# The first eight tiles of a graph kernel handled as two halves of four, with the attention vectors' products behind the first half

## The chip, the cores and the metric

The kernel runs on one core of one Trainium2 chip. The metric is the device time of one execution in microseconds. Five executions before the change gave a median of 1932.76 us, from 1931.08 to 1934.57 us.

The engines are named as in the profile: PE is TensorE (matrix products; PEld is its loading of weights), DVE is VectorE, ACT is ScalarE, POOL is GpSimd and SP is SyncE, which issues most of the DMAs here. A name with a small q behind it (SPq) is the queue of instructions of that engine. Each engine works through its own instructions strictly in order, and waits on semaphores for the others.

## What is computed

`x` holds 3125 nodes with 256 numbers each, `src` and `dst` the two ends of 103125 edges, sorted by `dst`. Four layers follow one another, each with a layer norm in front and a residual sum behind. The change lies at the start of the first, a three-layer graph attention:

```python
def _gat_layer(x, src, dst, W, al, ar, b, n_nodes):
    h = x @ W
    el = h @ al
    er = h @ ar
    e = jax.nn.leaky_relu(el[src] + er[dst], NEG_SLOPE)
    m = jax.ops.segment_max(e, dst, num_segments=n_nodes)
    ex = jnp.exp(e - m[dst])
    s = jax.ops.segment_sum(ex, dst, num_segments=n_nodes)
    alpha = ex / s[dst]
    out = jax.ops.segment_sum(alpha[:, None] * h[src], dst, num_segments=n_nodes)
    return out + b

x = x + _L0_gnn_ref(_layernorm(x, axis=-1), src, dst, ...)     # three _gat_layers
x = x + _L0_ffn_ref(_layernorm(x, axis=-1)[None], ...)[0]      # 16 experts, 2 for each node
x = x + _L1_gnn_ref(_layernorm(x, axis=-1), ...)
x = x + _L1_ffn_ref(_layernorm(x, axis=-1)[None], ...)[0]      # 8 experts, 1 for each node
```

## The kernel before

The nodes lie in 25 tiles of 128 (the last has 53), and two tiles make a group, so that there are 13 groups (`GROUPS`). The attention is computed densely: for every pair of tiles the number of edges between their nodes is counted into `counts`, and TensorE multiplies with these counts. Behind the layer norm, a tile needs its projection `h`, and two scores, which come out of the same product, because the weights `we` have two further columns, `W @ al` and `W @ ar`.

The front, which is what the change touches, is the part of `dense_attention` (line 1121) ahead of the loop over the three layers. In the order of the program it does this:

- `Locator` (line 1457) loads the first ends of the sorted list (an ACT DMA at line 1476) and makes two short lists of them on DVE (L1487, L1490). `load_nodes` loads `x` with six DMAs of four tiles and one for the last tile (L1668, L1671), on SP's queue: two in front of the weights' three DMAs (`attention_weights`, L1063 to L1065: `al` and `ar` into `wa`, `W` into `we`), the others behind them.
- `locator.find(0)` (line 1498) finds where the first part of the nodes begins in the list of edges: one large comparison on DVE (L1502), 33 small matmuls on PE (L1508), two small DVE operations (L1510, L1512), and two gathers of edges by POOL's own DMAs (L1523).
- `WARM` = 24 matmuls on PE follow (L1175). They multiply the comparison's result, so that they wait for L1502, and nothing reads what they make.
- `statistics(t0, n)` (line 1157) makes mean and variance of tiles on DVE (L1163, L1164). Those of tiles 4 and 5 come behind the comparison by a copy written for that (L1162).
- `spreads(t0, n)` (line 1166) makes the reciprocal spreads of some tiles: a square root on ACT (L1168) and a reciprocal on DVE (L1169).
- `turn(a)` (line 1178) normalises the two tiles of group a (L1184: the first on DVE, the second on POOL), transposes each with two PE matmuls into PSUM (L1188), and copies them back on ACT (L1190, `yT`).
- `products()` (line 1067) issues the DMA of the bias (L1068), and makes the two further columns of `we` in four DVE products with an accumulator each (L1074), behind a small copy that holds them back (L1071).
- The loop over the groups (line 1200) makes the statistics of tiles 8 to 24 in portions, their spreads in group 3 together with `locator.finish(0)` (DVE L1540 to L1550, ACT L1545, PE L1555, ACT L1558: it turns the gathered edges into keys for counting), turns the next group, and puts the present one: `Sources.put` (line 1103) multiplies on PE with `we` (L1111), clips the scores on DVE (L1114, `lr`), takes two exponentials on ACT (L1115, L1116), and scales the projection out of PSUM on ACT (L1118). From group 4 on each group also counts two pairs of windows (DVE L1594, PE L1606, ACT L1609).

The instructions of each engine are put in their order by a scheduler when the program is built. It starts from the order of the program and moves an instruction forward where its own times say that the engine would stand idle. The orders below are those of the built programs. Square root and exponential need different tables on ACT; a load of a table is inserted where the needed one isn't there.

Of the kernel before, what the change touches and what calls it, by code (L numbers as in the profile page):

```python
# [9 lines left out]
F32 = mybir.dt.float32  # L10
# [5 lines left out]
AF = mybir.ActivationFunctionType  # L16
OP = mybir.AluOpType
# [4 lines left out]
P = 128  # L22
# [4 lines left out]
D = 256  # L27
# [1020 lines left out]
EARLY = 8  # L1048
# [3 lines left out]
def attention_weights(tc, cp, one, layers, i, behind=None):  # L1052


    nc = tc.nc
    w, al, ar, b = layers[i]
    we = cp.tile([P, KD, D + 2], F32, name="we")
    at = cp.tile([P, 2, D], F32, name="wa")
    bt = cp.tile([P, D], F32, name="wb")
    if behind is not None:  # L1060
        for to in (we[:, 0], at[:, 0], at[:, 1], bt):
            nc.gpsimd.tensor_copy(to[:, 0:1], behind)
    nc.sync.dma_start(at[:, 0], spread(al, D))  # L1063
    nc.sync.dma_start(at[:, 1], spread(ar, D))
    nc.sync.dma_start(we[:, :, :D], w.rearrange("(k p) f -> p k f", p=P))  # L1065

    def products(behind=None):
        nc.sync.dma_start(bt, spread(b, D))  # L1068
        junk = one.tile([P, D], F32, name="wjunk")
        if behind is not None:  # L1070
            nc.vector.tensor_copy(junk[:, 0:1], behind)  # L1071
        for k in range(KD):
            for j in range(2):
                nc.vector.scalar_tensor_tensor(junk, we[:, k, :D], 1.0, at[:, j], op0=OP.mult, op1=OP.mult,  # L1074
                                               accum_out=we[:, k, D + j:D + j + 1])
    return we, bt, products
# [13 lines left out]
class Sources:  # L1090
# [9 lines left out]
        for to in (self.h[:, NT - 1], self.rho[:, NT - 1:], self.lr[:, :, NT - 1]):  # L1100
            self.nc.gpsimd.memset(to, 0.0)

    def put(self, pp, t, r, xTs, w, at=()):


        nc, n = self.nc, len(xTs)
        pss = []
        for i, xT in enumerate(xTs):
            ps = at[i] if i < len(at) else pp.tile([P, D + 2], F32, name="ps_m")
            for k in range(KD):  # L1110
                nc.tensor.matmul(ps[:r], xT[:, k], w[:, k], start=(k == 0), stop=(k == KD - 1))  # L1111
            pss.append(ps)
        for i, ps in enumerate(pss):
            nc.vector.tensor_scalar(self.lr[:r, :, t + i], ps[:r, D:], -HELD, HELD, op0=OP.max, op1=OP.min)  # L1114
        nc.scalar.activation(self.h[:r, t:t + n, D], self.lr[:r, 0, t:t + n], AF.Exp, scale=0.2)  # L1115
        nc.scalar.activation(self.rho[:r, t:t + n], self.lr[:r, 0, t:t + n], AF.Exp, scale=0.8)  # L1116
        for i, ps in enumerate(pss):
            nc.scalar.activation(self.h[:r, t + i, :D], ps[:r, :D], AF.Copy, scale=self.h[:r, t + i, D:])  # L1118


def dense_attention(tc, dram, counts, x_in, big, ident, eps, layers, src, dst, rows, high, make_router, over):
# [9 lines left out]
    nc = tc.nc  # L1131
    with tc.tile_pool(name="dw", bufs=1) as cp, tc.tile_pool(name="dwl", bufs=2) as wl, \
# [7 lines left out]
        we, bt, products = attention_weights(tc, wl, cp, layers, 0)  # L1140
        load_nodes(nc, x, x_in, EARLY)
        now = Sources(tc, big, small)
        with tc.tile_pool(name="dp", bufs=6) as pmp, tc.tile_pool(name="ds", bufs=2) as sp, \
# [10 lines left out]
            mv = small.tile([P, NT, 2], F32, name="mv")  # L1154
            rstd = small.tile([P, 2, NT], F32, name="rstd")

            def statistics(t0, n):
                for t in range(t0, t0 + n):
                    st = sp.tile([P, 6], F32, name="st")
                    if EARLY // 2 <= t < EARLY // 2 + 2:  # L1160

                        nc.vector.tensor_copy(st[:NHEAD, 0:1], locator.less[:NHEAD, 0, 0:1])  # L1162
                    nc.vector.bn_stats(st, x[:, t])  # L1163
                    nc.vector.bn_aggr(mv[:, t], st)  # L1164

            def spreads(t0, n):
                to = rstd[:, :, t0:t0 + n]
                nc.scalar.activation(to[:, 0], mv[:, t0:t0 + n, 1], AF.Sqrt, bias=eps)  # L1168
                nc.vector.reciprocal(to[:, 0], to[:, 0])  # L1169
# [3 lines left out]
            made = ap_.tile([P, 2, CHUNK], F32, name="acc")  # L1173
# [4 lines left out]
            def turn(a):  # L1178
                c, n = GROUPS[a]
                xTs = []  # L1180
                for j, q in enumerate(range(0, n, P)):
                    t, r = (c + q) // P, min(P, n - q)
                    xn = sp.tile([P, D], F32, name=f"y{j}")
                    (nc.gpsimd if j else nc.vector).tensor_scalar(xn, x[:, t], mv[:, t, 0:1], rstd[:, 0, t:t + 1],  # L1184
                                                                  op0=OP.subtract, op1=OP.mult)
                    to = turned[:, a % 2, j * D:(j + 1) * D]
                    for k in range(KD):
                        nc.tensor.transpose(to[:, k * P:(k + 1) * P], xn[:, k * P:(k + 1) * P], ident)  # L1188
                    xT = sp.tile([P, KD, P], F32, name=f"yT{j}")
                    nc.scalar.copy(xT, to.rearrange("p (k r) -> p k r", k=KD))  # L1190
                    xTs.append(xT[:, :, :r])
                return xTs

            statistics(0, EARLY)
            spreads(0, EARLY)
            xTs = turn(0)
            products(mv[:, EARLY - 1, 0:1])
            stats = list(range(EARLY, NT))
            ahead = list(pairs[0])
            for a, (c, n) in enumerate(GROUPS):  # L1200
                pairs_now = [ahead.pop(0) for _ in range(min(2, len(ahead)) if 2 * a >= EARLY else 0)]
                for pair in pairs_now:
                    counter.make(pair, 0)
                while stats and len(stats) > (NT - EARLY) * (EARLY // 2 - a - 2) // (EARLY // 2 - 1):
                    statistics(stats.pop(0), 1)
                if 2 * a == EARLY - 2:
                    spreads(EARLY, NT - EARLY)
                    locator.finish(0, pp, mv[:, NT - 1, 0:1])
                later = turn(a + 1) if a + 1 < len(GROUPS) else None
                now.put(pp, c // P, min(P, n), xTs, we, [made[:, a % 2, :D + 2]])  # L1210
                xTs = later
                for pair in pairs_now:
                    counter.add(kp, pair)
# [4 lines left out]
            for i in range(3):  # L1218
# [10 lines left out]
                else:  # L1229
                    nxt = Sources(tc, big, small)  # L1230
                    we_n, bt, products = attention_weights(tc, wl, cp, layers, i + 1, now.rho[:, NT - 1:])
# [81 lines left out]
                now = nxt  # L1313
# [441 lines left out]
```

## Time and profile before

| | |
|---|---|
| median of five executions | 1932.76 us |
| the profiled execution | 1931.46 us |
| its span (first to last instruction) | 1929.7 us |
| mean granted TensorE clock | 0.993 |
| PE busy | 1864.6 us, 97% of the span |
| DVE, ACT, POOL busy | 1002.6, 748.6, 297.3 us |
| PE busy from 0 to 13 us | 0 us of 13 |
| PE busy from 23 to 29 us and from 29 to 35 us | 4.36 us and 3.96 us of 6 |
| PE busy from 35 to 58 us | 22.53 us of 23 |

The times below count from the start of the span. In a row of the timeline the first number is the start, the second the time that the instructions in it took from the first start to the last end; then engine, line, operation, what is written and read, and the count; in brackets stands how long the engine was idle before, and what ended that. Instructions of one engine overlap by some ten nanoseconds, so that the step from one start to the next is a little shorter than the duration.

### The profile page before, as it was taken

Reading aid. Unit: us, or ns where it says so; the run is one execution under the profiler, and the core shown is the slowest. Engines: PE = TensorE matmul, PEld = TensorE weight load, DVE = VectorE, ACT = ScalarE, POOL = GpSimd, SP = SyncE. Lnnn points to the kernel's source line nnn. Section 1 sums busy time; section 2 is a strip of 40 time slices with the busy share of each in tenths; the row PEclk is TensorE's granted clock in tenths of the full one; section 3 lists DMA queues with packets and bytes.
Section 4 is the critical chain, followed back from the end, with each engine's and each line's share of the span. In section 5 each row is a group of like instructions: output and inputs, shape, how many; then the busy total and the mean of one; then the engine's idle time right before and its main releaser. Section 6 shows DMA issues by size and latency. Waiting matters only on the chain.

```text
span 1929.7 us, 27975 instructions
## 1 busy us (share of the span) xinstructions
PE 1864.6 (97%) x9466; PEld 1480.3 (77%) x9466; DVE 1002.6 (52%) x2909; ACT 748.6 (39%) x2254; POOL 297.3 (15%) x454
## 2 busy tenths in 40 slices
PE   6999999999999999999999989999989999999998
PEld 4788888887788888788888757777668887455887
DVE  6899888785555555567777722222235222334222
ACT  4867777672000011122222211111127999544221
POOL 4200000000000000022323322233310000132122
PEclk9999999999999999999999989999999999999999
DMA  4101113575100000011111165667540000633764
GB/s 124 32 21 53 41 67 121 209 282 236 58 1 1 1 1 3 9 56 45 44 45 45 39 200 151 188 176 240 125 105 1 1 1 1 229 137 143 215 209 137
DMA packets 103577, 182.96 MB, mean 95 GB/s; under 512 B 10054, under 2 KB 72741, under 8 KB 103392
## 3 DMA queue, kind: packets, MB, share of 16 engines
q1 hardware_dynamic: 72268, 124.32, 18.9%
q0 software_dynamic: 16016, 34.28, 6.5%
q10 hardware_dynamic: 15138, 22.44, 3.6%
q8 instruction: 80, 1.31, 0.3%
q14 instruction: 75, 0.61, 0.1%
HBM read 92.93 MB, written 90.17 MB: 95 GB/s over the span
## 4 chain that ended last, share of the span: by engine, by line
PE 87%; issue 5%; DMA 3%; ACT 3%; DVE 2%; POOL 1%; SPq 0%; ACTq 0%; POOLq 0%; DVEq 0%
PE acc L1263 40%; PE ps_h L762 9%; PE acc L1382 7%; PE ps_H L901 4%; PE ps_o L775 4%; PE ps_y L995 4%; PE acc_c L1606 4%; PE ps_m L1111 3%; DMA out_dram<-y,who 2%; PE ps_h L807 1%; PE ps_m L1365 1%; PE ps_rows L945 1%; PE acc L1385 1%; PE ps_cols L1022 1%; PE ps_o L819 1%
## 5 line engine op out<-in xcount | busy, mean ns | idle before, releaser
L1263 PE MATMUL acc<-big,pm 128*128 128x257 f32 (+1 forms) x3750 | 871.0, 382 | 4.7 <-DVE pm L1260 4.3
L1263 PEld LDWEIGHTS acc<-big,pm 128*128 128x128 f32 (+1 forms) x3750 | 680.5, 187 | 110.8 <-DVE pm L1260 9.6
L1260 DVE SCALAR_TENSOR_TENSOR pm<-tau,rho,counts 128x256 f32<-128x256 f32 (+1 forms) x975 | 437.3, 467 | 158.7 <-PE acc L1263 155.9
L762 PE MATMUL ps_h<-xsT,w 128*128 128x384 f32 x512 | 167.8, 486 | 0.5 <-ACT xsT L738 0.5
L1382 PE MATMUL acc<-msg,cr 128*128 128x512 f32 (+1 forms) x625 | 157.9, 403 | 0.1
L1594 DVE TENSOR_TENSOR ohk<-iota_k,key 128x1200 f16<-128x1200 f16 x196 | 151.5, 774 | 6.3 <-PE acc_c L1606 6.2
L762 PEld LDWEIGHTS ps_h<-xsT,w 128*128 128x128 f32 x512 | 97.2, 190 | 65.1 <-ACT xsT L738 0.7
L1382 PEld LDWEIGHTS acc<-msg,cr 128*128 128x128 f32 (+1 forms) x625 | 114.7, 185 | 29.2 <-ACT cr L1378 1.2
L1378 ACT ACTIVATE cr<-counts 128x256 fp32r<-128x256 uint8 (+1 forms) x325 | 130.5, 402 | 14.4 <-PE acc L1382 7.0
L1606 PE MATMUL acc_c<-ohk,ohs 128*128 128x200 f16 x1176 | 130.0, 249 | 1.4 <-ACT ohs L1591 1.4
L1590 ACT ACTIVATE far<-iota_s,low 128x128 f16<-128x128 f16 x360 | 123.6, 398 | 6.8 <-POOL far L1588 2.5
L1606 PEld LDWEIGHTS <-ohs 128*128 128x128 f16 x1176 | 105.0, 98 | 26.2 <-ACT ohs L1591 1.8
L995 PE MATMUL ps_y<-t_wd,hsT 128*128 x480 | 108.8, 380 | 0.4 <-ACT hsT L1023 0.4
L765 ACT ACTIVATE silu<-ps_h 128x384 f32<-128x384 f32 x64 | 31.4, 491 | 199.5 <-PE ps_h L762 199.5
L766 DVE TENSOR_TENSOR hid<-silu,ps_h 128x384 f32<-128x384 f32 x64 | 35.5, 554 | 136.3 <-PE ps_h L762 126.4
L1609 ACT CAST counts<-acc_c 128x400 uint8<-128x400 f32 x196 | 93.3, 481 | 32.7 <-PE acc_c L1606 32.0
L1243 ACT ACTIVATE tau<-ps_m 128x256 f32<-128x256 f32 (+1 forms) x39 | 14.1, 370 | 215.5 <-PE ps_m L1241 197.3
L995 PEld LDWEIGHTS ps_y<-t_wd,hsT 128*128 128x128 f32 x480 | 88.8, 190 | 11.6 <-ACT hsT L1023 0.6
L780 POOL DMA_INDIRECT sums<-y,who x48 | 75.0, 1562 | 131.4 <-DVE y L778 121.8
L901 PE MATMUL ps_H<-big,t_w 128*128 128x512 f32 (+1 forms) x224 | 93.1, 552 | 0.8 <-ACT H L903 0.5
L775 PE MATMUL ps_o<-w,hid 128*128 128x256 f32 x384 | 86.9, 379 | 0.0
L1594 DVE TENSOR_TENSOR ohs<-iota_s,low 128x512 f16<-128x512 f16 (+1 forms) x196 | 83.5, 426 | 0.0
(298 smaller groups left out, 1931.5 us busy)
## 6 DMA issues: line engine op xcount, KB each, us to landing
rows<-empty SPq DMA_DIRECT2D x16, 2564.0 KB, 15.0
w<-in_L_ffn_w_dram ACTq DMA_DIRECT2D x42, 512.0 KB, 7.5
hs<-rows SPq DMA_DIRECT2D x29, 641.0 KB, 4.1
w<-in_L_ffn_w_dram SPq DMA_DIRECT2D x30, 512.0 KB, 4.9
rows<-empty SPq DMA_DIRECT2D x16, 516.0 KB, 4.3
t_wd<-in_L_ffn_Wd_dram SPq DMA_DIRECT2D x8, 1024.0 KB, 12.5
xs<-rows SPq DMA_DIRECT2D x15, 387.0 KB, 5.2
bias<-in_L_ffn_bd_dram SPq DMA_DIRECT2D x30, 128.0 KB
```

The costliest lines, as they stand in the source:

```text
L762: nc.tensor.matmul(ps, w[:, k, j * P:(j + 1) * P], xsT[:, k], start=(k == 0), stop=(k == KD - 1))
L775: nc.tensor.matmul(ps, hid[:, j, q * P:(q + 1) * P], o[:, j], start=(j == 0), stop=(j == nh - 1))
L901: nc.tensor.matmul(ps[:, :n], a[:, k, j * P:(j + 1) * P], xnT[:, k, c:c + n], start=(k == 0), stop=(k == KD - 1))
L995: nc.tensor.matmul(ps, hsT[:, j], d[:, ds(e, 1), j, :].rearrange("p o f -> p (o f)"), start=(j == 0), stop=(j == nh - 1))
L1260: nc.vector.scalar_tensor_tensor(pm[:, :n], tau[:, :n], now.rho[:, s:s + 1], edges[:, s, :n], op0=OP.max, op1=OP.mult)
L1263: nc.tensor.matmul(acc[:r, j, :D + 1], pm[:, q:q + r], now.h[:, s], start=(s == 0), stop=(s == NT - 1))
L1378: nc.scalar.activation(cr[:, :n], edges[:, s, :n], AF.Copy, accum_out=seen[:, a * NT + s:a * NT + s + 1])
L1382: nc.tensor.matmul(acc[:r, j].rearrange("p h d -> p (h d)"), cr[:, q:q + r], msg[:, s].rearrange("p h d -> p (h d)"), start=(s == 0), stop ...
L1590: nc.scalar.activation(far[:, i], self.iota_s, AF.Abs, scale=-1.0, bias=self.low32[:, pair, i:i + 1])
L1594: nc.vector.tensor_tensor(to[:, i:].rearrange("p t (x u) -> p t x u", u=2), iota.rearrange("p (x u) -> p x u", u=2)[:, None].to_broadcast( ...
L1606: nc.tensor.matmul(acc[:, u], ohs[:, i], ohk[:, i], start=(t == 0), stop=(t == TW - 1))
L1609: nc.scalar.copy(to[:, :, d0 % PAIR:d0 % PAIR + 2 * WIN].rearrange("p s (u d) -> p u s d", u=2), acc.rearrange("p u (s d) -> p u s d", d=WIN))
```

## The change

`spreads` and `statistics` of the first eight tiles are made in two halves, tiles 0 to 3 and 4 to 7. `products` now stands behind the statistics of tile 3, not of tile 7, and ahead of the first `turn`. A tile `zero` is made out of the reciprocal spread of tile 7 times 0.0, and the exponentials of groups 0 and 1 take it as their bias, so that they come behind the second square root.

```diff
-    def put(self, pp, t, r, xTs, w, at=()):
+    def put(self, pp, t, r, xTs, w, at=(), zero=0.0):
...
-        nc.scalar.activation(self.h[:r, t:t + n, D], self.lr[:r, 0, t:t + n], AF.Exp, scale=0.2)
-        nc.scalar.activation(self.rho[:r, t:t + n], self.lr[:r, 0, t:t + n], AF.Exp, scale=0.8)
+        nc.scalar.activation(self.h[:r, t:t + n, D], self.lr[:r, 0, t:t + n], AF.Exp, bias=zero, scale=0.2)
+        nc.scalar.activation(self.rho[:r, t:t + n], self.lr[:r, 0, t:t + n], AF.Exp, bias=zero, scale=0.8)
...
-            statistics(0, EARLY)
-            spreads(0, EARLY)
+            half = EARLY // 2
+            statistics(0, half)
+            spreads(0, half)
+            products(mv[:, half - 1, 0:1])
             xTs = turn(0)
-            products(mv[:, EARLY - 1, 0:1])
+            statistics(half, EARLY - half)
+            spreads(half, EARLY - half)
+
+            zero = small.tile([P, 1], F32, name="zero")
+            nc.vector.tensor_scalar(zero, rstd[:, 0, EARLY - 1:EARLY], 0.0, None, op0=OP.mult)
...
-                now.put(pp, c // P, min(P, n), xTs, we, [made[:, a % 2, :D + 2]])
+                now.put(pp, c // P, min(P, n), xTs, we, [made[:, a % 2, :D + 2]],
+                        zero if 2 * a < half else 0.0)
```

In the built programs the first instructions of DVE stand in these orders (by the lines of the kernel before; "tile 0" and so on say which tile an operation works on):

```
before                                after
L1487, L1490  lists of find           L1487, L1490  lists of find
L1163, L1164  statistics, tiles 0-3   L1163, L1164  statistics, tiles 0-3
L1502         comparison of find      L1071         copy ahead of the products
L1162 x2      copies                  L1074         product 1 (waits for we, al)
L1163 x2      statistics, tiles 4, 5  L1169         reciprocal, tiles 0-3
L1510, L1512  place of the edges      L1074         product 2 (waits for ar)
L1163, L1164  tiles 6, 7, 8, 9        L1184         normalise tile 0
  with L1071, L1074 x4, L1169 (0-7)   L1074         product 3
  and L1184 (tile 0) among them       L1502         comparison of find
L1163, L1164  tiles 10-24             L1074         product 4
  with L1184 (tiles 2, 4, 6) and      L1162 x2      copies
  L1114 x3 among them                 L1184         normalise tile 2
L1540-L1550   finish                  L1510, L1512  place of the edges
                                      L1163, L1164  tiles 4-24
                                        with L1169 (4-7), zero, L1184
                                        (tiles 4, 6) and L1114 x2 among them
                                      L1540-L1550   finish
```

On POOL, the normalising of tiles 1 and 3 (L1184) moves from behind the gathers of find (L1523) and the memsets and patterns around them to the front of the memsets L1618 and L1622; the memset of L1519 for `src_p` moves behind the gathers. On ACT one square root of eight becomes two of four, side by side, ahead of the first `yT` copy. On PE the 33 matmuls of find and the 24 of `WARM` stay first, and the transposes of tile 0 come behind them, as before; further on some L1188 and L1111 change places with each other and with L1555 and L1606. The order on SP is unchanged. Behind the front no order differs, and no instruction is added or removed other than the second square root, the second reciprocal and `zero`.

## Prediction

> **What bounds the kernel now.** I read the page first, then the chain of waits of the first 70 us, the timeline of the front engine by engine, and the DMA view. PE carries the whole kernel, but not from the start:
>
> ```profile
> PE 1864.6 (97%) x9466; PEld 1480.3 (77%) x9466; DVE 1002.6 (52%) x2909; ACT 748.6 (39%) x2254; POOL 297.3 (15%) x454
> ```
>
> Behind the front no order changes, so what the front ends later or earlier, the kernel ends later or earlier. The chain of waits (start, duration, what) says what sets the front's beginning:
>
> ```profile
> 11.43 1.74 DVE counts L1502
> 13.17 0.04 issue
> 13.21 2.91 PE acc_c L1508 x33
> 16.12 6.64 PE acc L1175 x24
> 22.76 0.23 PE acc L1188 x2
> ```
>
> The reader is to see that the first transposes (L1188) don't wait for the normalised tile. They stand on PE behind the 33 matmuls of find and the 24 of WARM, and all these wait for one DVE instruction, L1502. Tile 0 is normalised at 19.59, 2.8 us before PE is free for it at 22.43. Any delay of L1502 delays PE one for one; an earlier tile gains nothing while the 57 matmuls are in front of it.
>
> On DVE the change puts a copy, three of the four products, a reciprocal and a normalising in front of L1502. What they cost (timeline, DVE):
>
> ```profile
> 11.35 1.81 DVE L1502 TENSOR_TENSOR counts<-counts 125x3234 f16<-125x3234 f16 x1
> ...
> 18.04 0.41 DVE L1074 SCALAR_TENSOR_TENSOR wjunk<-we,wa 128x256 f32<-128x256 f32 x1
> 18.37 0.08 DVE L1074 DVE_READ_ACCUMULATOR wjunk<-we,wa 128x1 f32 x1
> ...
> 19.19 0.18 DVE L1169 RECIPROCAL rstd<-rstd 128x8 f32<-128x8 f32 x1
> 19.29 0.37 DVE L1074 SCALAR_TENSOR_TENSOR wjunk<-we,wa 128x256 f32<-128x256 f32 x1
> ...
> 19.59 0.88 DVE L1184 TENSOR_SCALAR y<-big,mv,rstd 128x256 f32<-128x256 f32 x1
> ...
> 21.54 0.38 DVE L1184 TENSOR_SCALAR y<-big,mv,rstd 128x256 f32<-128x256 f32 x1
> ```
>
> A product takes 0.33 us from its start to the next start (18.04 to 18.37, again 0.30 from 19.29 to 19.59), the reciprocal 0.10 (19.19 to 19.29).
>
> The products also need `we` and `wa`. At 18 us these had long landed; at 11.4 us they need not have:
>
> ```profile
> 1.87 0.50 SPq L1063 DMA_DIRECT2D wa<-in_L_gnn_al_dram  x1
> ...
> 2.94 0.94 SPq L1065 DMA_DIRECT2D we<-in_L_gnn_W_dram  x1
> ...
> wa<-in_L_gnn_al_dram SPq DMA_DIRECT2D x1, 128.0 KB, 9.6
> ...
> 10.00:13.00 3.00, 0.00 (x0) 0.00 (x0) 3.00 (x9) 0.00 (x0) 0.00 (x0) 1.00 1.10 348
> ```
>
> `al` lands 9.6 us after its issue, at 1.87 + 9.6 = 11.47. Behind it on the queue come `ar` (131 kB) and `we` (262 kB). The last row is the stretch from 10 to 13 us (PE, PEld, DVE, ACT, POOL busy; clock, DMA share, GB/s): 348 GB/s, POOL idle.
>
> **The change part by part.**
>
> *Wait for the weights (added).* 393 kB at 348 GB/s are 1.13 us, so `we` lands at about 12.60. The mean of the first four tiles is ready at 11.43, so DVE stands still for some 1.1 us. Ends: 11.47, if all three land together; 15.6, if the loads of tiles 8 to 15 (1.05 MB), issued behind them, share the bandwidth: (0.393 + 1.05) MB / 348. I take 12.60, because a queue whose first load landed at 9.56 (the chain's first DMA) and whose third at 11.47 works nearly in order. Behind the waiting product stand L1502, and for it PE, and for PE the gathers of POOL.
>
> *Work in front of L1502 (moved).* Three products at 0.33, the reciprocal 0.10, one normalising 0.38: 1.47 us. The reciprocal's square root on ACT (0.30 us for eight columns) runs inside the wait for `we`. The normalising took 0.88 once, so this part is 1.47 to 1.97; I take 1.47, as the later ones, with POOL at the same work beside them, took 0.41, 0.38 and 0.41 (at 23.02, 25.67, 31.76). L1502 starts at 12.60 + 1.47 = 14.07 in place of 11.35: **+2.72 us**.
>
> *PE.* 33 and 24 matmuls as before, 2.91 and 6.64 us, all 2.72 later. The 24 ran at two rates: some 16 from 15.98 to 21.2 (0.33 us each), the last eight at about 0.17. If the switch keeps its place in the span, the 24 take 2.5 us slowly and 2.8 fast, 1.3 less; if it comes too late for all, 24 x 0.33 = 7.9, 1.3 more. I take 0, since what PE does ahead of the switch is unchanged. The Trainium skill ("TensorE: Matmul & The Clock Gate", Part 1) says that the clock doubles after a busy window of about 3.4 us and that the windows run freely, without regard to the kernel. The two rates agree; by the page the sum would change by chance from run to run, up or down by less than the bounds above, and would stay 2.72 in the mean.
>
> *POOL.* L1184 of tiles 1 and 3 go to the front of its queue: about 13.0 to 15.7 (1.32 us each, 3.96 for three at 21.62). The memsets behind (0.95 + 1.17 + 0.42 and small ones) end at about 18.5; the gathers can start when `at` is ready, at 16.51 + 2.7 = 19.2. So POOL's new work is hidden by 0.7 us; without that cover the gathers come later, and they have 4 us more: landing 5.3 to 6.5 us after issue means by 26.7, and finish's L1543, at 29.27 before, comes at 31 or later. The memset of `src_p` ends near 23 instead of 6.5, and SP's L1520 at 16.86 waits for it, with the small loads of the gate and four fills of `sums` behind; nothing in the front reads those. Cost 0.
>
> *Second square root, zero.* The second root waits for tile 7's statistics at about 21; ACT has nothing to do until the first `yT` copy at 23.02 + 2.7. The biased exponentials come behind, so that the exponentials' table isn't loaded between the roots; without that, two more loads of 1.28 us. Cost 0.
>
> *DVE behind find.* 21 statistics at 0.44 (0.66 + 0.22 for two), two normalisings, and small ones: some 11 us from L1510 to the last aggregate, against 12.9 before (16.16 to 29.07). This 1.9 us gains nothing if ACT is what finish and group 1 wait for:
>
> ```profile
> 29.03 0.38 ACT L1190 COPY yT<-acc 128x256 f32<-128x256 f32 x1
> 29.42 1.28 ACT L1168 ACT_TABLE_LOAD   x1
> 30.72 0.31 ACT L1168 ACTIVATE rstd<-mv,eps 128x17 f32<-128x17 f32 x1
> 31.05 1.28 ACT L1115 ACT_TABLE_LOAD   x1
> ```
>
> ACT works without a gap from 27.85 to 33.9, and has the same operations ahead of 32.34 after the change. Near 33 PE takes group 2's products ahead of group 3's transposes, which could save 0 to 0.6 us (before, L1111 started at 33.34, behind transposes that waited 2 us). I take 0, because PE is full from 35 us on and the number of its instructions is the same.
>
> **Sum:** +2.7 us. The profiled execution (1931.46, its span 1929.7) would take 1934.2; the median, 1.3 above that execution, 1932.76 + 2.7 = **1935.5 us**.
>
> **The rivals.**
>
> *L1502 is slowed by POOL (slower).* In the kernel before POOL does nothing while L1502 runs; now it normalises two tiles. For it: the 0.88 against 0.38 of L1184, with POOL's memsets beside it, a ratio of 2.3. L1502 would take 4.2 in place of 1.81, +2.4, in all +5.1: 1937.9 us. It decides from 1.2 us of stretch on, where the sum passes 0.2%. Against it:
>
> ```profile
> 39.56 0.77 DVE L1594 TENSOR_TENSOR ohk<-iota_k,key 128x1200 f16<-128x1200 f16 x1
> 39.70 1.73 POOL L1184 TENSOR_SCALAR y<-big,mv,rstd 128x256 f32<-128x256 f32 x1 [2.43 <-PE acc L1188]
> ```
>
> The same kind of operation keeps its 0.77 there, and POOL is the one that loses (1.73 against 1.22). The Trainium skill ("GPSIMD Engine Reference", Specifications) says that POOL shares its ways into SBUF with VectorE and contends with operations of two SBUF inputs. Such are L1502 and the products; by the rule alone the sum would be the 5.1 of this rival, by the row 2.7.
>
> *The front catches up.* The 1.9 us that DVE saves count, if group 1 waits for the last statistics: 2.7 - 1.9 = +0.8, 1933.6 us. Against it: ACT's unbroken queue above; the statistics ended 0.35 us before the table load, not behind it.
>
> *Faster, as the order in the program suggests.* Tile 0 is normalised at about 13.7, not 19.59, and if PE could use it the front would start 5.9 us sooner: 1926.9. In the built order PE can't: L1508 and L1175 stand in front. That the change does not bring the first projections forward is thus part of my forecast.
>
> **How the numbers follow.** Forecast 0.58, POOL rival 0.22, catching up 0.14, faster 0.06. A measurement of this kernel can tell about 0.2%, 3.9 us, from no change. The forecast's own range is 1933.7 to 1937.2: down by the early landing (1.13) or the early clock (1.3) or the 0.6, up by the late clock (1.3) or the slow L1184 (0.5); I give it 0.18 above 1936.6 and 0.40 within. Slower: 0.18 + 0.22 = 0.40; same: 0.40 + 0.14 = 0.54; faster: 0.06. The range reaches down to 1933.0, below the catching up, and up to 1938.2, the POOL rival; a landing at 15.6 and the faster case stay outside.
>
> **What would show it.** DVE idle before the first L1074, ended by the DMA of `we`, till about 12.6; L1502 at 14.1 with 1.8 us; L1508 at 15.9; the first L1188 near 25.2; ACT's exponential of group 1 near 35; the first full PE stretch 2.7 us later. I am wrong if L1502 starts before 13, if it takes over 3 us, or if what follows the first transposes closes the gap.

## The result and the profile after

| | before | after |
|---|---|---|
| median of the runs beside each other | 1933.08 us (44 runs) | 1935.82 us (24 runs) |
| lowest to highest | 1930.12 to 1936.69 us | 1933.09 to 1938.22 us |
| ratio, 95% interval | | 1.0014, 1.0008 to 1.0019 |
| the profiled execution / its span | 1931.46 / 1929.7 us | 1935.23 / 1933.5 us |

The changed kernel is slower by 2.7 us (1.5 to 3.7 us by the interval), 0.14% of the time. That is less than the 0.2% by which the prediction tells a difference from none, and is seen only because so many runs stand beside each other. So the reading rests on marks in the traces (when a certain instruction starts), and the medians test it. From line 1218 of after on, an instruction stands 7 lines further down than in before: L1502 is L1509, L1508 is L1515, L1510 is L1517.

The busy times tell nothing: PE's is the same to 0.3 us.

```profile
PE 1864.3 (96%) x9466; PEld 1479.6 (77%) x9466; DVE 1002.6 (52%) x2911; ACT 749.5 (39%) x2255; POOL 298.6 (15%) x454
```

The timeline of DVE in after shows the step that the sum was built on (start, time, engine and line, operation; in brackets the idle time before and what ended it):

```profile
11.81 0.15 DVE L1071 COPY wjunk<-mv 128x1 f32<-128x1 f32 x1
13.08 0.42 DVE L1074 SCALAR_TENSOR_TENSOR wjunk<-we,wa 128x256 f32<-128x256 f32 x1 [1.11 <-DMA we<-in_L_gnn_W_dram]
...
13.43 0.17 DVE L1169 RECIPROCAL rstd<-rstd 128x4 f32<-128x4 f32 x1
13.54 0.42 DVE L1074 SCALAR_TENSOR_TENSOR wjunk<-we,wa 128x256 f32<-128x256 f32 x1
...
13.90 0.64 DVE L1184 TENSOR_SCALAR y<-big,mv,rstd 128x256 f32<-128x256 f32 x1
14.46 0.41 DVE L1074 SCALAR_TENSOR_TENSOR wjunk<-we,wa 128x256 f32<-128x256 f32 x1
...
14.80 1.83 DVE L1509 TENSOR_TENSOR counts<-counts 125x3234 f16<-125x3234 f16 x1
...
24.87 0.18 DVE L591 TENSOR_SCALAR off<-real 128x25 f32<-128x25 f32 x1 [1.59 <-POOL real L587]
...
31.30 0.17 DVE L1164 BATCH_NORM_AGGREGATE mv<-st 128x2 f32<-128x6 f32 x1
```

The first product waits 1.11 us for the DMA of `we`, and everything behind it on DVE waits along. The comparison starts at 14.80 in place of 11.35, and itself takes 1.83 us, as before. The two last rows are for later: a wait that the prediction did not see, and the end of the statistics.

POOL normalises its tiles at the same time (timeline, POOL):

```profile
13.71 4.30 POOL L1184 TENSOR_SCALAR y<-big,mv,rstd 128x256 f32<-128x256 f32 x2 [10.19 <-DVE rstd L1169]
```

PE follows the comparison, and the first transposes come behind its 57 matmuls (timeline, PE):

```profile
16.69 2.91 PE L1515 MATMUL acc_c<-one,counts 125*98 125x1 f16 x33 [16.69 <-DVE counts L1509]
19.46 5.89 PE L1175 MATMUL acc<-counts 125*98 125x392 f16 x24
25.19 0.38 PE L1188 MATMUL acc<-ident,y 128*128 128x128 f32 x2
```

They wait for nothing: the tile was normalised more than ten microseconds earlier, at 13.90. ACT's stretch around the second square root answers to the one shown of before (timeline, ACT):

```profile
31.55 0.37 ACT L1190 COPY yT<-acc 128x256 f32<-128x256 f32 x1
31.93 1.28 ACT L1168 ACT_TABLE_LOAD   x1
33.22 0.31 ACT L1168 ACTIVATE rstd<-mv,eps 128x17 f32<-128x17 f32 x1
...
33.81 1.28 ACT L1115 ACT_TABLE_LOAD   x1
35.10 0.30 ACT L1115 ACTIVATE big<-lr,zero 128x2 f32<-128x2 f32 x1
```

The table load comes right behind a copy, without idle time, as it did before. All of it is 2.5 to 2.8 us later than in the trace of before that the prediction was made from: the root of the 17 other tiles at 33.22 in place of 30.72, group 1's exponential at 35.10 in place of 32.34.

### The profile page after: what moved, and what is told of

Read it like the earlier page. It is cut to its first block, busy times and chain, and to the rows that moved or that the text cites. A ratio compares the mean times of both kernels' runs of the same rounds, so it can differ in the third digit from the quotient of the medians.

```text
span 1933.5 us, 27974 instructions
## 1 busy us (share of the span) xinstructions
PE 1864.3 (96%) x9466; PEld 1479.6 (77%) x9466; DVE 1002.6 (52%) x2911; ACT 749.5 (39%) x2255; POOL 298.6 (15%) x454
## 5 line engine op out<-in xcount | busy, mean ns | idle before, releaser
L1616 ACT CAST counts<-acc_c 128x400 uint8<-128x400 f32 x196 | 93.2, 480 | 33.9 <-PE acc_c L1613 33.2
```

Of the source, the lines that this page charges most:

```text
L1616: nc.scalar.copy(to[:, :, d0 % PAIR:d0 % PAIR + 2 * WIN].rearrange("p s (u d) -> p u s d", u=2), acc.rearrange("p u (s d) -> p u s d", d=WIN))
```

## The experiments

Five marks were read in each trace, as starts in microseconds of the span: the comparison; the first transposes (L1188); the square root of tiles 8 to 24 (L1168); the first keys for counting (`ohs`, DVE); and the first `tau` on ACT (L1243 before), which opens the first attention layer. The ratio is to the runs of the kernel before that were taken beside it, with its 95% interval; it is an estimate from all these runs, and differs from the quotient of the two medians by up to 0.0003.

| kernel | comparison | transposes | root | keys | tau | ratio |
|---|---|---|---|---|---|---|
| before | 11.35 | 22.60 | 30.72 | 36.94 | 66.58 | |
| before, e8 | 11.35 | 21.91 | 30.31 | 36.91 | 67.00 | one trace |
| before, e11 | 11.35 | 21.46 | 30.31 | 36.54 | 66.18 | one trace |
| after | 14.80 | 25.19 | 33.22 | 39.62 | 69.74 | 1.0014 (1.0008 to 1.0019) |
| e1, only the products | 14.52 | 25.07 | 33.20 | 39.56 | 69.87 | 1.0012 (1.0003 to 1.0021) |
| e2, only the halves | 12.81 | 23.20 | 31.24 | 37.62 | 67.74 | 0.9998 (0.9989 to 1.0007) |
| e3, products behind find | 12.75 | 23.84 | 31.06 | 37.45 | 67.58 | 0.9991 (0.9982 to 1.0000) |
| e10, the same again | 12.78 | 23.00 | 30.21 | 36.60 | 66.73 | 0.9994 (0.9985 to 1.0003) |
| e4, comparison thrice | 11.30, three times | 25.34 | 33.46 | 40.07 | 70.17 | 1.0010 (1.0001 to 1.0019) |
| e5, find first | 11.45 | 22.88 | 30.91 | 37.30 | 67.41 | 0.9995 (0.9986 to 1.0004) |
| e6, find first, WARM 8 | 11.27 | 18.67 | 30.58 | 34.99 | 66.18 | 0.9994 (0.9985 to 1.0003) |
| e9, find first, WARM 16 | 11.21 | 20.32 | 30.91 | 35.33 | 66.30 | 0.9991 (0.9982 to 1.0000) |
| e7, before, WARM 8 | 11.35 | 20.61 | 34.06 | 39.78 | 70.82 | 1.0007 (0.9999 to 1.0016) |

One thousandth is 1.9 us. The three traces of the same kernel before show how far a mark moves by itself: `tau` by 0.4 us to either side of their mean, 66.59. The spans of these three are 1929.7, 1931.9 and 1931.7 us, so what follows `tau` scatters by up to 2.4 us more, and a median of eleven runs tells about 1.8 us.

### Which half of the change costs the time

**e1** puts the products behind tile 3 in the kernel before, and leaves everything else of the change out:

```diff
-            statistics(0, EARLY)
+            statistics(0, EARLY // 2)
+            products(mv[:, EARLY // 2 - 1, 0:1])
+            statistics(EARLY // 2, EARLY - EARLY // 2)
             spreads(0, EARLY)
             xTs = turn(0)
-            products(mv[:, EARLY - 1, 0:1])
```

> The kernel before, with the products alone moved behind the statistics of tile 3; spreads, normalising and exponentials as before. In the built order the copy and all four products stand in front of the comparison of find. My theory (the products' wait for we, and the DVE work in front of the comparison, pass one for one into the time): the first product waits for we until about 12.6 to 12.9 us, the comparison starts some 2.5 us later than before (1.1 of wait, 4 x 0.34 of work), and the median is 2.5 us above the kernel before (ratio 1.0013, from 1.0008 to 1.0018). Rival, that the normalising beside POOL or the two halves carry the loss: within 0.7 us of the kernel before.

The timeline of DVE in e1 has the same wait:

```profile
12.76 0.42 DVE L1074 SCALAR_TENSOR_TENSOR wjunk<-we,wa 128x256 f32<-128x256 f32 x1 [1.11 <-DMA we<-in_L_gnn_W_dram]
...
14.52 1.84 DVE L1503 TENSOR_TENSOR counts<-counts 125x3234 f16<-125x3234 f16 x1
```

The wait for `we` is 1.11 us again, now with four products behind it, and the comparison is 3.17 us late. All later marks are those of after, and the ratio is too (that `tau` agrees as well is partly chance, as the part on chance shows). The move of the products alone carries the loss.

**e2** keeps the halves, the second root and `zero`, and moves the products back:

```diff
             spreads(0, half)
-            products(mv[:, half - 1, 0:1])
             xTs = turn(0)
             statistics(half, EARLY - half)
             spreads(half, EARLY - half)
+            products(mv[:, EARLY - 1, 0:1])
```

> The changed kernel, with the products back behind the statistics of tile 7: the two halves, the early normalising and the bias stay. In the built order a reciprocal and the normalising of tiles 0 and 2 stand in front of the comparison. My theory: the comparison starts about 1.3 us later than before (0.35 for the square root, 0.1, two normalisings at 0.4 to 0.6 with POOL beside them), no wait for we; the median is about 1.3 us above the kernel before (1.0007, from 1.0002 to 1.0011). Rival, that the products are harmless and the halves carry the loss: 2.7 us above. Rival, that the early halves gain by themselves: below the kernel before.

DVE in e2, timeline:

```profile
11.77 0.18 DVE L1169 RECIPROCAL rstd<-rstd 128x4 f32<-128x4 f32 x1 [0.36 <-ACT rstd L1168]
11.99 0.90 DVE L1184 TENSOR_SCALAR y<-big,mv,rstd 128x256 f32<-128x256 f32 x2
12.81 1.83 DVE L1509 TENSOR_TENSOR counts<-counts 125x3234 f16<-125x3234 f16 x1
```

Without the products the square root on ACT is no longer covered (0.36 us of waiting), and two normalisings stand in front of the comparison: it is 1.46 us late. The marks follow by 0.5 to 1.2 us, and the median shows no loss: my 1.3 us lie at the upper edge of its interval.

**e3** and, measured again, **e10** hold the products back behind the comparison, and leave the rest of the change:

```diff
-            nc.vector.tensor_copy(junk[:, 0:1], behind)
+            nc.vector.tensor_copy(junk[:behind.shape[0], 0:1], behind)
...
-            products(mv[:, half - 1, 0:1])
+            products(locator.less[:locator.rows, 0, 0:1])
```

> The changed kernel, with the copy ahead of the products reading the result of the comparison, so that the products come behind it. In front of the comparison stand the reciprocal and two normalisings, as in the run with the halves only. My theory: the comparison starts about 1.3 us later than before, the median is 1.3 us above the kernel before, and 1.4 below the changed kernel. Rival, that the place of the products is not what costs: as the changed kernel, 2.7 us above before.

> The run with the products behind the comparison once more: its median lay 1.7 us below the kernel before (ratio 0.9982 to 1.0000), where its marks said 0.5 to 1.2 above. If the early normalising gains by itself, 0.9991 again; if that was scatter, 1.0000 to 1.0006, and marks as in its first profile (first transposes 0.7 to 1.9 us behind the kernel before, by the switch of PE's rate).

The comparison starts at 12.75 and 12.78. I had expected the 1.4 us of its delay to reach the time, some 1.3 us, and it didn't: the intervals of e3 and e10 end at 0.0 and +0.6 us. Part of the answer is in the marks, which are only 1.0 and 0.1 us later at `tau`. Two things in the traces shorten the way there.

First, in before the second pair of transposes can have to wait for tile 1, which POOL finishes normalising at 23.1. Two further traces of before show it (timeline, PE; e8, then e11):

```profile
21.91 0.38 PE L1188 MATMUL acc<-ident,y 128*128 128x128 f32 x2
23.10 0.44 PE L1188 MATMUL acc<-ident,y 128*128 128x128 f32 x2 [0.81 <-POOL y L1184]
```

```profile
23.10 0.44 PE L1188 MATMUL acc<-ident,y 128*128 128x128 f32 x2 [1.26 <-POOL y L1184]
```

Whenever PE gets there before 23.1, it waits: from the first transposes to the root it is 8.40 and 8.85 us in these two, against 8.12 in the first trace, which had no such wait. With the halves, POOL is done with tiles 1 and 3 before 16 in e2, e3 and e10, and this floor is gone.

Second, e3 and e10 take 7.22 and 7.21 us over the same stretch. The missing floor is not the reason, since e2 and e5, which don't have it either, take 8.04 and 8.03. The reason is the built order on ACT: in e3 and e10 the exponentials' table is loaded behind the third copy, in the others behind the fourth, for which ACT must wait. ACT in e3, timeline:

```profile
26.32 0.37 ACT L1190 COPY yT<-acc 128x256 f32<-128x256 f32 x1 [0.72 <-PE acc L1188]
26.71 1.28 ACT L1115 ACT_TABLE_LOAD   x1
```

The medians of e2, e3 and e10 lie lower still than their marks. Taken together, the 22 executions of e3 and e10, which are one kernel, lie 0.9 us below those of before beside them in the mean (95% interval 0.3 to 1.5 us below). So this kernel may be a little faster than before; what gives that is not shown.

### Does a late comparison alone explain it

**e4** makes find's first comparison three times in a row in the kernel before. Nothing else moves, no weight is waited for, and POOL does what it did:

```diff
-            nc.vector.tensor_tensor(
-                less[:rows].rearrange("p q (w u) -> p q w u", u=2),
+            for _ in range(3 if j == 0 else 1):
+                nc.vector.tensor_tensor(
+                    less[:rows].rearrange("p q (w u) -> p q w u", u=2),
...
```

> The kernel before, with the comparison of find made three times into the same place: 2 x 1.75 = 3.5 us more of DVE work in front of PE's first matmul, and nothing else moved. My theory, one for one: 3.5 us above the kernel before (1.0018, from 1.0013 to 1.0023), every mark behind the first transposes 3.5 us later but for the chance of the clock's switch. Rival, that the front catches up behind the first transposes: less than 1.5 us above.

DVE and then PE in e4, timeline:

```profile
11.30 5.57 DVE L1503 TENSOR_TENSOR counts<-counts 125x3234 f16<-125x3234 f16 x3
```

```profile
16.92 2.91 PE L1509 MATMUL acc_c<-one,counts 125*98 125x1 f16 x33 [16.92 <-DVE counts L1503]
...
25.34 0.38 PE L1188 MATMUL acc<-ident,y 128*128 128x128 f32 x2
```

The two further comparisons make PE start 3.71 us late. Against the mean of before the root is 3.01 us later and `tau` 3.58 us, part of which is the clock's (see the part on chance). So a delay of DVE ahead of these 57 matmuls passes through the front for the greater part, though not one for one: where tile 1 holds up PE in before, as in e8 and e11, 0.8 to 1.3 us of it are absorbed. The median says +1.9 us (0.2 to 3.7): above nothing, with the 3.5 us that I expected at its upper edge.

**e5** is e3 with the reciprocal held behind the comparison too, so that nothing new stands in front of it:

```diff
             statistics(0, half)
+            nc.vector.tensor_copy(rstd[:locator.rows, 0, 0:1], locator.less[:locator.rows, 0, 0:1])
             spreads(0, half)
-            products(mv[:, half - 1, 0:1])
+            products(locator.less[:locator.rows, 0, 0:1])
```

> The run with the products behind the comparison, and the first four square roots held behind it as well (a copy of its result into the tile that they write), so that nothing stands in front of the comparison. My theory: the comparison is back at 11.3 us as in the kernel before, the first transposes at 22.4 (but for the clock's switch, 0.9 either way), and the median is as before, within 0.7 us; the last statistics may end 1 to 2 us sooner without gain, as ACT's queue is what group 1 waits for. Rival, that the halves are worth something by themselves once nothing delays the comparison: 1.5 us or more below the kernel before.

DVE in e5, timeline:

```profile
11.45 1.81 DVE L1510 TENSOR_TENSOR counts<-counts 125x3234 f16<-125x3234 f16 x1
...
13.55 0.42 DVE L1074 SCALAR_TENSOR_TENSOR wjunk<-we,wa 128x256 f32<-128x256 f32 x1
```

The comparison is back where it was, the product no longer waits, the transposes and the root are within 0.3 us of the first trace of before, and the ratio is 1 within its interval, which lies wholly below that of after. Undoing the delay undoes the loss. Whether the halves win something by themselves e5 doesn't decide: its interval, from 2.7 us below before to 0.8 above, holds my 0.7 us as well as the rival's 1.5. The last statistics didn't end sooner, as I had expected, but at 30.02 in place of 29.07, behind a wait of 1.70 us for POOL's pattern (L591).

### Is it the 24 matmuls that hide a gain

With tile 0 ready so early, fewer matmuls of `WARM` could let PE use it. **e6** and **e9** are e5 with `WARM = 8` and `WARM = 16`, **e7** is the kernel before with `WARM = 8`. The matmuls left out are read by nothing.

> The same with 8 matmuls of WARM in place of 24. If the 24 are what keeps an early tile from being of use: the first transposes come 2.7 us behind the last matmul of find, near 18.8, and with the statistics ending near 27 the square root of the 17 tiles (30.72 in the kernel before) comes at 27.5 to 28.5: 2 to 3.5 us below the kernel before (0.9982 to 0.999). Rival, that PE's slow clock takes it back (transposes and products at half rate until the switch): within 1 us of the kernel before.

> The run with the comparison first, with 16 matmuls of WARM: 8 matmuls (1.3 to 2.6 us) less in front of the first transposes, and the rate of PE switched before or soon after them. If the transposes' start is what sets the front, 1 to 2 us below the kernel before (0.9990 to 0.9995); if the 17-tile root or the order that the scheduler makes of the exponentials takes over, as in the runs with 8, within 0.7 us of the run with 24.

> The kernel before with 8 matmuls of WARM in place of 24 and nothing else. Tile 0 is normalised at 19.6 and product 4 made at 20.7, so that PE can start at some 20.5 in place of 22.4, and the statistics still end near 29: 1 to 1.5 us below the kernel before if that is what counts (0.9992 to 0.9995); as before if the slow clock takes it back. Against the run with find first and 8 it tells what the early halves add.

In e6 the first transposes start at 18.67, 3.9 us ahead of the first trace of before. ACT's timeline shows where that goes:

```profile
27.80 0.30 ACT L1115 ACTIVATE big<-lr,zero 128x2 f32<-128x2 f32 x1
...
29.29 1.28 ACT L1168 ACT_TABLE_LOAD   x1
30.58 0.31 ACT L1168 ACTIVATE rstd<-mv,eps 128x17 f32<-128x17 f32 x1
```

Group 1's exponential is 4.5 us earlier than in before (27.80 against 32.34), since the scheduler has put it ahead of the square root, but the root, which I had expected at 27.5 to 28.5, starts within 0.3 us of where it did in all three traces of before. The statistics, expected near 27, ended at 29.55, so that it could have started one microsecond earlier at most. The first keys are 1.8 and 1.5 us early in e6 and e9, but `tau`, at 66.18 and 66.30, is inside the scatter of before: from about 33.2 to 36.6 us the granted clock was down to half in both (the row is below), and the stretch from the keys to `tau` took 31.19 and 30.97 us in place of 29.64. Three microseconds of a busy PE at half the clock are worth some 1.5 us by my estimate, so that this by itself takes most of the lead back in these two traces. The ratios, 0.9994 and 0.9991, have intervals that reach 1.0003 and 1.0000: a gain is possible, and not shown; e9's fits both of the cases that I had set against each other.

In e7 the marks are later instead; the median's interval, 0.9999 to 1.0016, still holds no loss. PE's timeline, and ACT's:

```profile
23.10 0.69 PE L1188 MATMUL acc<-ident,y 128*128 128x128 f32 x2 [1.82 <-POOL y L1184]
23.58 1.93 PE L1111 MATMUL acc<-we,yT 128*128 128x258 f32 x4
```

```profile
34.06 0.31 ACT L1168 ACTIVATE rstd<-mv,eps 128x17 f32<-128x17 f32 x1
```

PE reaches tile 1 early, stands still until POOL is done with it at 23.10, and is then slow: 1.93 us for four products, 1.04 in before and in after. It stays so until about 28 us. The root is 3.3 us later than in the first trace of before, and not all of it is PE's slow pace: group 0's exponential is 2.0 us later (29.80 against 27.85), and the other 1.4 us come from ACT's built order, which in e7 has a copy of group 1 that waits for PE, and its exponentials, ahead of the root.

### What chance does to the front

**e8** and **e11** are the kernel before, unchanged, for one more trace each.

> The kernel before once more, for its profile alone: the 24 matmuls of WARM took 6.45 us from first to last start in the profile before and 5.5 to 6.3 in the others. If the switch of their rate comes by chance, this execution has another length between 5.4 and 7; if it hangs on the kernel, 6.45 again.

> The kernel before for a third profile: the 24 matmuls of WARM take between 5.4 and 7 us, at another place of the switch than 21.4 and 19.9 us of the span; from the first transposes to the root of 17 tiles 8.0 to 8.4 us; from there to the first exponential of the layers (tau) 36 to 36.7 us.

The first transposes start at 22.60, 21.91 and 21.46 in three executions of one program. The windows of `WARM`'s matmuls alone tell why. Columns: the stretch, its length, PE's busy time and count, PEld's, clock, DMA share, GB/s; before, e8, e11:

```profile
15.90:21.40 5.50, 5.42 (x17) 3.57 (x18) 1.00 0.87 273
21.40:22.60 1.20, 1.20 (x9) 0.74 (x6) 1.00 0.67 225
```

```profile
15.90:19.90 4.00, 3.91 (x12) 2.52 (x13) 1.00 0.98 300
19.90:21.80 1.90, 1.90 (x13) 1.35 (x11) 1.00 0.73 214
```

```profile
15.90:18.90 3.00, 2.91 (x9) 1.95 (x10) 1.00 0.97 312
18.90:21.40 2.50, 2.50 (x16) 1.76 (x14) 1.00 0.70 216
```

In each, the first row is the slow pace (5.42 / 17, 3.91 / 12 and 2.91 / 9 us for a matmul: 0.32 to 0.33) and the second the fast one (0.13 to 0.16; the counts of each pair add up to one or two more than 24, as a matmul on a border counts in both). The switch comes 5.5, 4.0 and 3.0 us behind the same start. The clock column says 1.00 throughout: here it does not show the change of pace, the counts do. e8 and e11 ran on chips 0 and 1, so these traces alone don't tell chance from chip; but e5, on chip 0 like e8, took 6.79 us from the start of `WARM` to the transposes where e8 took 5.92. In e11 two of my figures missed: from the first transposes to the root it took 8.85 us, by the wait for tile 1, and from there to `tau` 35.87.

Further on the clock changes again, and there the column shows it. One row each of before, e8 and e6 (columns: the stretch, its length, busy time and count of PE, PEld, DVE, ACT and POOL, clock, DMA share, GB/s):

```profile
34.00:36.00 2.00, 1.47 (x11) 1.09 (x10) 0.56 (x2) 1.54 (x7) 0.91 (x1) 1.00 0.04 8
```

```profile
34.00:36.00 2.00, 1.91 (x10) 1.41 (x9) 0.57 (x2) 1.26 (x6) 0.51 (x1) 0.50 0.00 0
```

```profile
34.00:36.00 2.00, 2.00 (x7) 1.58 (x7) 0.73 (x3) 1.38 (x6) 1.46 (x2) 0.50 0.04 8
```

In e1, e4 and e6 to e9 the granted clock is down to half for some three microseconds between 33 and 43 us; in the other seven traces it is not. In e1, e4 and e8 this follows a wait of PE of 1.98 us, but before and e11 have the same wait (1.98 and 1.97) and keep the clock. From the root to `tau` it is 35.86 us in before and 35.87 in e11, and 36.67 to 36.71 in e1, e4 and e8: 0.8 us more. The kernels with the halves and 24 matmuls (after, e2, e3, e5, e10) take 36.50 to 36.52 there at full clock, 0.65 us more than before; whether this comes from their order of instructions or from something else in them was not tested. That e1 and after meet at `tau` has these two different reasons.

## Why the prediction was right, point by point

**The wait for the weights.** Taken as 1.13 us, measured as 1.11 in after and again in e1. That these agree to 0.02 us is partly chance, since 1.13 was the transfer and 1.11 the idle time: `al` landed at 11.77 in after and 11.47 in e1, and the product started 1.3 us later in both. This fits a queue that works nearly in order; of the two ends, all three loads at once and bandwidth shared with the loads behind, neither came.

**The work in front of the comparison.** Taken as 1.47 us, measured as 1.72 (13.08 to 14.80). A product took 0.35 us from start to start in place of 0.33, the reciprocal 0.11, and the normalising 0.56 (13.90 to 14.46) in place of 0.38. This last was the term that was mis-sized: it was priced by later rows of its kind, while tile 0's own row in before had 0.88. Of the three rows named for the price, with POOL said to be at the same work beside them, the one at 25.67 had POOL idle (from 25.58 to 26.30). The upper end of the whole part in the prediction was 1.97.

**The start of the comparison.** Taken as 14.07, measured as 14.80, or 3.45 us later instead of 2.72. Of the 0.73 us between, 0.25 is the work just named, 0.14 the distance from the point where the comparison could have started to the landing of `we` (1.39 us; 1.25 was taken, from 11.35 to 12.60), and 0.34 is chance: the first ends of the edges landed later in this execution (DVE's short lists started at 9.46 in place of 8.96), and the statistics behind them at 9.94 in place of 9.59. In e1 they started at 9.63, and the first product at 12.76.

**PE.** Taken as unchanged, with 1.3 us to either side for the clock. The 57 matmuls took 8.50 us from the first start to the transposes (16.69 to 25.19), 0.89 us less than in the first trace of before (13.21 to 22.60). The further traces of before, with 8.69 and 8.25 us, show that the place of the switch does this. It pays back what the comparison lost beyond the forecast, so that the first transposes start at 25.19, where 25.2 was forecast. Two misses of opposite sign met there; the mechanism is shown by e1, e4 and e5, not by that agreement. The Trainium skill ("TensorE: Matmul & The Clock Gate", Part 1) says that the window of about 3.4 us runs freely, so that the switch falls differently in each run. That the switch fell 3.0, 4.0 and 5.5 us behind the start of `WARM` agrees with that, though not with the half microsecond to either side that the page gives.

**POOL and SP.** Taken as hidden, and hidden, though not by the margin given. The two normalisings on POOL took 4.30 us, not the 2.7 taken (1.38 the first, 2.93 the second, which ran beside most of the comparison); its memsets ended at 20.5 instead of 18.5, and the gathers started about 0.2 us behind the point at which they could have. The 0.7 us of cover was gone. It cost nothing further on: the gathers were issued at 20.73 and 22.28 and landed 4.4 and 3.6 us later, while finish began at 31.51, behind the statistics. SP's wait grew too, because the memset of `dst_p`, which the prediction left in its place, moved behind the normalisings as well (waits of SP's queue: what waits, what for, us, times, longest):

```profile
SPq L1527 <- POOL dst_p L1526: 5.0, 1, 5.0
```

Nothing in the front needs what stands behind it.

**DVE behind find.** Taken as 11 us from L1510 (now L1517) to the last aggregate, and 1.9 us shorter than before. It took 11.8 (19.64 to the end at 31.47), for the reason in the last DVE rows shown: DVE stood 1.59 us before L591, which needs a pattern that POOL makes and that had slipped behind POOL's late gathers. The prediction looked for what waits for POOL on SP and missed this one on DVE. It was covered, by 0.46 us: the last aggregate ended at 31.47, ACT came to the table load at 31.93.

**ACT's queue.** Taken as what sets group 1, so that DVE's saving gains nothing. From the first transposes to the root it was 8.03 us in after, 8.12 in the first trace of before, e4 8.12, e1 8.13. Group 1's exponential is 2.76 us later than in that trace, 3.03 later than in the mean of the three. Two steps were missing. The trace that the prediction was made from has no wait for tile 1; in e8 and e11 that wait takes up 0.8 and 1.3 us, so that a delay of PE does not always pass one for one. And behind the root, where the new order on PE was said to save 0 to 0.6 us or nothing, the kernels with the halves took 0.65 us longer to `tau`. So the mechanism holds up to the root, and that the median moved by just the 2.7 of the sum is in part luck.

**The rivals.** That POOL slows the comparison: it took 1.83 us with POOL at work all through it, 1.81 with POOL idle. POOL is the one that loses: the tile that it normalised beside most of the comparison took 2.93 us (2.32 to 2.33 in e2, e3 and e10, where less of the comparison was left), the one ahead of it 1.38, where 1.32 was the mean of before. The Trainium skill ("GPSIMD Engine Reference", Specifications) names DVE's operations with two inputs in SBUF among those that contend with POOL; in these rows the cost of it fell on POOL. That the front catches up: ACT's rows leave no gap to catch up in, and the marks behind, the first keys at +2.82 us and `tau` at +3.15 against the mean of before, show none. That it is faster because tile 0 comes early: tile 0's normalising started at 13.90, the transposes took it at 25.19. Even with the matmuls in between cut down (e6, e9), the gain didn't reach `tau` in the two traces.

**What stays open.** At `tau`, after is 3.15 us late, and the median 2.7; e1 has 3.28 and 2.3 (0.6 to 4.1), e4 3.58 and 1.9. The medians of e1 to e5 all lie about a microsecond or more below their marks at `tau`, that of e3 beyond its interval. The three traced executions of before are a likely reason: they took 1.3, 0.9 and 1.8 us less than the median of the runs of before beside them, those of e1 to e5 and e10 between 1.0 us less and 1.9 more, so that the marks of before are probably early ones. No single experiment beats the kernel before beyond its interval. But e3 and e10 are one kernel, and together they do, by 0.9 us in the mean, and e5, e6 and e9 lie 1.1 to 1.6 us lower in the mean too: the halves may be worth about a microsecond once the products are out of the comparison's way. Against it stands e2, at 0.2 us above in the mean, and the marks don't show where such a gain would come from.

## What to carry to other kernels

An instruction that is moved forward on an engine that works in order brings its own waits along, and hands them to everything behind it: in e1 four small products, 1.8 us of work, made the comparison that PE was waiting for 3.2 us late, because 1.4 us more went by until their weights had landed. Before making an input ready earlier, look at what stands in front of its consumer on the *consumer's* engine; here 57 matmuls did, and an input ready more than ten microseconds early gained nothing. Where an effect is a thousandth of the time, compare starts of named instructions in several traces of the same kernel, see whether the traced executions are typical of its runs, and let the medians confirm the sign.

## What the runs showed of the hardware

- One program's matmuls went from 0.33 us to half of that 3.0, 4.0 and 5.5 us behind the same start in three executions. The transposes behind them started at 21.46, 21.91 and 22.60 us, over a microsecond of scatter.
- After a wait of PE of 1.98 us the granted clock fell to 0.50 for about three microseconds in e1, e4 and e8, and stayed at 1.00 in before and, after 1.97, in e11. From the root to `tau` the first three took 0.8 us longer.
- With two normalisings on POOL beside them, DVE's half-precision comparison kept its time (1.83 against 1.81 us). Of DVE's own single-precision normalisings one took 0.64 us and one 0.43, against 0.38 to 0.41 in the later rows of before, and POOL's second took 2.93, against 1.32 in the mean of before.
- Eight warm-up matmuls, a wait of 1.80 us, one pair of transposes and a wait of 1.82 us left PE slow to about 28 us in e7 (1.93 us for four products, 1.04 later); in e6, with eight matmuls as well and a single wait of 1.56 us, four products took 1.04 from 21.17 on. One trace of each doesn't tell whether the waits or the place of the clock's switch made the difference.
